# Linear attention and a sparse FFN in one kernel: some input tiles transposed through HBM instead of on TensorE, two tiles normalized on ScalarE, and finer dependences for the FFN's products

## The chip, the cores and the metric

The kernel runs on one core of a Trainium2 chip. The metric is the device time of one execution in microseconds (us). A profiled execution also gives the span from the first to the last instruction. Below, PE is TensorE, DVE is VectorE, ACT is ScalarE, POOL is GpSimd and SP is SyncE, whose queue issues nearly all DMAs.

## The reference

All is fp32. `_layernorm` has no weights.

```python
x = L0_attn_x                                       # (2, 1024, 512)
x = x + _layernorm(attn(_layernorm(x), Wq, Wk, Wv, Wo))
x = x + _layernorm(ffn(_layernorm(x), w_gate, w_up, w_down))

# attn: 16 heads of 128, 4 key/value heads; q and k rotated (RoPE), then elu(.) + 1
state = state + k_s[..., :, None] * v_s[..., None, :]      # scan over 1024 positions
z = z + k_s
out = einsum('bhe,bhed->bhd', q_s, state) / (einsum('bhe,bhe->bh', q_s, z) + EPS)
return out.reshape(...) @ Wo.T

# ffn: 512 -> 2048 -> 512
h = silu(x @ w_gate) * (x @ w_up)
h_sparse = h with the 2 largest of every 4 (by magnitude) kept, the rest zero
return h_sparse @ w_down
```

## The kernel before

**Attention.** The 1024 positions are cut into 8 chunks of 128. The two batch entries of one chunk make a "tile pair", so there are eight pairs, 0 to 7, in `xt[n]`. The heads are done in two passes of eight, so there are 16 steps `n`: pair `n % 8`, pass `n // 8`. One step of the main loop issues the Q and K/V products of step `n + 1` (`q_products`, `kv_products`), four groups of scores and outputs of step `n` (`scores`, `attend`), and the output projection of step `n - 1` (`o_products`).

**Products.** A product of 2 x 2 blocks is done with seven block products and sums of operands ahead of them (`chain`, `FACTORS`). They run in the order 1, 2, 6, 5, 7, 4, 3, in PSUM banks of three kinds: "a" (one buffer in the attention part), "b" and "e" (two each). After products 1, 6 and 7, ACT copies bank "b" out (L528), and DVE adds the copy to what stands in "a" or "e" (L539). In the trace the banks are called `ca`, `cb` and `ce`.

**x.** `step_normalize(n)` takes the layernorm of a pair on DVE (statistics L656, L661; the square root on ACT L665; L667; then the normalization L185, in place). `step_input(n, b, kind)` transposes x of one batch entry with four PE transposes (L498) into a bank. ACT copies it out (L691, L697) into the first three of the seven blocks of a tile `xf`, and DVE makes the other four (L700, L704). `xf` is stored to HBM (L707) for the second pass, which loads it again. The kernel calls `step_input(n + 2, ...)` twice in step `n`, late in the step.

**The other transposes.** From some point on q features and the attention outputs are transposed by `moved`: DVE transposes 32 x 32 blocks (L630) into a tile `blocks` of three buffers, the tile is stored to HBM (`qb`, `ob`; L636) and comes back in four loads with the blocks in their new places (`qT`, `of`; L643). The first few q tiles and the output (step 0, group 3) go over PE and bank "a" instead (`q_transposed`, copies L855; `o_transposed`, copy L1032).

**FFN.** Four blocks of 512 rows (`m`), 2048 columns in four groups (`jb`). Each `gate(m, jb)` and `up(m, jb)` is a chain whose seven products take factors of x, made by `ffn_input(m)`: the first three are views of the transposed tile (`fxr`), three are DVE sums in the tile `fxt` (L1717), one is a POOL sum in place (L1719); all four are signalled as `fxf`. `sparsify` makes the masks and the factors of h on DVE (`ht` L1507, `g` L1465), with two Abs passes on ACT (L1459) and a sum on POOL (L1510). `down(m)` is the last product (L1527).

**Who sets the order.** The kernel is written for a manual schedule: each engine executes its instructions in the order in which the program issues them. PE's order is written out in the main loop and in `ffn_order`. For all other engines a small planner (`Plan`) decides: processes yield requests such as `("dve", 0.8, rank)`, which is an engine, a planned length and a rank, or wait for a named signal, and the planner runs them by planned time. Planned lengths and signals move instructions on DVE, ACT, POOL and SP; real waits on the chip follow from the data.

Of the kernel before, what the change touches and what calls it, by code (L numbers as in the profile page):

```python
# [111 lines left out]
def kernel(  # L112
# [54 lines left out]

    fb_dram = [dram.tile([P, 4 * P], F32, name=f"fb{tt}") for tt in range(4)]
    y_dram = [dram.tile([P, B, DM], F32, name=f"y{c}") for c in range(NC)]
    x2_dram = [dram.tile([P, B, DM], F32, name=f"x2_{c}") for c in range(NC)]  # L170
# [453 lines left out]

    def moved(src, through, new, name, *names):


        yield "dve", 0.8
        t = qp.tile([P, 4, 4, 32], F32, tag="blocks", name="blocks", bufs=3)
        nc.vector.transpose(  # L630
            out=t.rearrange("p b i r -> p i b r"),
            in_=src.rearrange("p i (b d) -> p i b d", d=32),
        )
        yield 0.2
        yield "sp", 0.44
        nc.sync.dma_start(out=through, in_=t.rearrange("p b i r -> p (b i r)"))  # L636
        yield plan.transfer(256)
        for n in names:
            yield n
        for b in range(4):  # L640
            yield "sp", 0.44
            t = t if b else new()
            nc.sync.dma_start(  # L643
                out=t[b * 32 : (b + 1) * 32],
                in_=through.rearrange("(u d) (b e) -> b d u e", u=4, b=4)[b],
            )
            landing = plan.transfer(64)
        yield landing + 1.5
        plan.signal(name)
# [22 lines left out]
    def step_normalize(n, root=None, rank=1):  # L672
        yield "x", n
        scales = yield from layernorm_pair([xt[n][:, b, :] for b in range(B)], B, "a", root, rank)
        for b in range(B):
            yield "dve", 0.56, rank
            normalize(xt[n][:, b, :], xt[n][:, b, :], *scales[b])
            plan.signal(("xn", n, b))

    def step_input(n, b, kind):  # L680
# [29 lines left out]

        plan.spawn((first, second)[b]())

    def step_input_again(n):
# [79 lines left out]
    def kv_products(n):  # L793
# [18 lines left out]
        def v21(b, name):  # L812
# [9 lines left out]
            project(weights[n // NC][0], n),  # L822
            lambda i: [("xf", n), ("w", n // NC, 0, i)],
            (qp, "keep256", 2),
# [39 lines left out]
    def q_products(n):  # L864
# [20 lines left out]
        def q21(b, name):  # L885
# [6 lines left out]
            project(weights[n // NC][1], n),  # L892
            lambda i: [("xf", n), ("w", n // NC, 1, i)],
            (qp, "keep512", 2),
# [128 lines left out]

    def o_transposed(n, i):

        plan.need(("divided", n, i), *o_free(n, i))
        pt, name = transposed(o.pop((n, i)), "a", ("divided", n, i))

# [9 lines left out]
    def o_sums(n):  # L1038
# [11 lines left out]

        yield "dve", 0.8
        nc.vector.tensor_tensor(of[n, 3], of[n, 3], of[n, 0], ALU.subtract)
        plan.signal(("of", n, 3, "sum"))
        yield "dve", 0.8
        nc.vector.tensor_tensor(factor(n, 4, 1), of[n, 2], of[n, 3], ALU.subtract)
# [185 lines left out]
    def first_factors():  # L1241
# [3 lines left out]
        xnT = ffn["xnT"].rearrange("p c (w t) -> p c w t", t=32)  # L1245
        xfs[0] = ffn_factors(t, xnT, nc.vector)
        plan.signal(("fxr", 0))
        plan.signal(("fxf", 0))
# [3 lines left out]
    ORDER = (1, 2, 6, 5, 7, 4, 3)  # L1252
    wgu_loaded = set()

    def landed(length, name):
# [10 lines left out]
    def ffn_order(gate, up, down, begin, end, finish):  # L1266
# [18 lines left out]
        for k, times in ((0, 2), (1, 1), (0, 3)):  # L1285
            run(live[k], times)
        live.reverse()
        for m in range(NM):
            for jb in range(1 if m else 2, NJB):
                queue += [partial(gate, m, jb), partial(up, m, jb)]  # L1290
            if m == 1:
                live += [one() for one in queue[0:2]]
                del queue[0:2]
            weave()
            end(m)
            products = down(m)
            if m + 1 == NM:
                finish()
                run(products, 11)
                break  # L1300
            g = gate(m + 1, 0)
            if m == 0:
                run(g, 5)
            if m != 1:
# [43 lines left out]
    def gate_or_up(m, jb, which, places):  # L1348
        def multiply(b, i, start):
# [8 lines left out]
            multiply,  # L1358
            lambda i: [("fxr" if i < 3 else "fxf", m), ("gu", m, jb, which, i)],
            (pool["keeps"], "keep", 4),  # L1360
# [303 lines left out]
    def ffn_input(m):  # L1664
# [48 lines left out]
        t = pool["xs"].tile([P, 3, 2, 256], F32, tag="fxt", name="fxt")  # L1713
        v = t.rearrange("p i k (w t) -> p i k w t", t=32)
        for k, i0, i1 in ((0, b12, b11), (1, b22, v[:, 0]), (2, b21, v[:, 1])):
            yield "dve", 0.75, 0
            nc.vector.tensor_tensor(v[:, k], i0, i1, ALU.subtract)  # L1717
        yield "pool", 1.45
        nc.gpsimd.tensor_tensor(b12, b22, b12, ALU.subtract)  # L1719
        xfs[m] += [v[:, 0], v[:, 1], b12, v[:, 2]]  # L1720
        plan.signal(("fxf", m))

    E = mybir.EngineType
    with tc.manual_schedule(engines={E.PE, E.Pool, E.SP, E.DVE, E.Activation}):
# [66 lines left out]
        for n in range(STEPS):  # L1791
# [20 lines left out]
            if n + 2 < STEPS:  # L1812
                if n + 2 < NC:
                    plan.spawn(step_normalize(n + 2, ("root", n)))
                else:
                    plan.spawn(step_input_again(n + 2))
# [20 lines left out]
            else:  # L1837
# [5 lines left out]
                if n == 1:  # L1843
                    scores(1, 0)
                    q_transposed(1, 1)
                    o_transposed(0, 3)
            run(kvp, 1)
# [27 lines left out]
            else:  # L1875
# [6 lines left out]
                outputs(2)  # L1882
                if n + 2 < NC:
                    step_input(n + 2, 0, "a")
                run(opr, 2)
# [4 lines left out]
            if n > 0:  # L1890
                k_transposed(n + 1)
                run(opr, 1)
                if n + 2 < NC:
                    step_input(n + 2, 1, "a")
                outputs(3)
# [116 lines left out]
```

## Time and profile before

| | |
|---|---|
| median of 3 runs | 1292.43 us (1290.6 to 1292.5) |
| profiled execution, its own time | 1291.52 us |
| its span | 1289.8 us, mean granted PE clock 0.998 |
| busy: PE, DVE, ACT, POOL | 98%, 67%, 35%, 26% of the span |
| PE waits in all of the 1289.8 us | 23.7 us (span less busy) |
| DMA | 252.57 MB, mean 196 GB/s; 62.1% of the 16 engines' span on SP's queue |
| one step in the middle of the attention part | 42.94 us (the same score from 132.06 to 175.00 us) |

A row of a timeline reads: start us, us, engine, line, operation, output<-input, shape, count, and in brackets the idle time of the engine before it with what ended it. A line number is that of the kernel before. PE rows overlap, since matmuls are pipelined: what one costs is the distance to the next start.

### The profile page before, as it was taken

The numbers are of one execution on the slowest core, as the hardware profiler recorded it, in microseconds if no ns is written. First come the engines' busy times: TensorE is split into PE (matmuls) and PEld (weight loads), VectorE is DVE, ScalarE is ACT, GpSimd is POOL, SyncE is SP. The second block draws the span as 40 slices with busy tenths as digits, with TensorE's granted clock in tenths as the row PEclk, the third lists the DMA queues.
The fourth block names the chain that finished last, engine by engine and source line by source line (L and its number), as shares of the span: only waits on it lengthen the run. The fifth ranks groups of instructions, "written<-read, shape, count | busy, mean of one in ns | idle before, by whom it ended". The sixth has DMA issues, their size and how long they took to land. (4 is left out here: it accounts for less than half of the span.)

```text
span 1289.8 us, 17309 instructions
## 1 busy us (share of the span) xinstructions
PE 1266.1 (98%) x5868; PEld 1016.6 (79%) x5868; DVE 868.6 (67%) x1521; ACT 456.4 (35%) x905; POOL 341.1 (26%) x261
## 2 busy tenths in 40 slices
PE   7899999999999999999999999999999999999998
PEld 4567777777777777777788887888888888888886
DVE  7987876777666787678764488416981687426763
ACT  3644454444334344444443333113220333023211
POOL 4634442532232454455431101001100110110010
PEclk9999999999999999999999999999999999999999
DMA  7375678659656866676485499267547756465312
GB/s 253 116 243 197 202 232 275 208 201 313 217 191 208 295 224 229 224 235 206 156 242 166 122 261 261 92 199 217 155 124 228 237 153 199 147 184 175 114 37 95
DMA packets 280295, 252.57 MB, mean 196 GB/s; under 512 B 19216, under 2 KB 239376, under 8 KB 277520
## 3 DMA queue, kind: packets, MB, share of 16 engines
q1 hardware_dynamic: 278832, 249.51, 62.1%
q10 hardware_dynamic: 1376, 1.97, 0.4%
q8 instruction: 47, 0.77, 0.2%
q14 instruction: 40, 0.33, 0.1%
HBM read 179.83 MB, written 71.57 MB: 195 GB/s over the span
## 5 line engine op out<-in xcount | busy, mean ns | idle before, releaser
L528 ACT COPY u<-cb 128x512 f32<-128x512 f32 (+1 forms) x252 | 126.6, 503 | 477.3 <-PE cb L250 171.1
L1078 PE MATMUL cb<-wo,of 128*128 128x256 f32 x512 | 121.1, 379 | 0.0
L736 PE MATMUL cb<-wq,xf 128*128 128x512 f32 x256 | 120.4, 593 | 0.3 <-ACT u L528 0.3
L250 PE MATMUL cb<-fxnT,wgu 128*128 128x256 f32 x512 | 116.9, 379 | 2.3 <-issue 2.3
L250 PE MATMUL cb<-fxt,wgu 128*128 128x256 f32 x512 | 116.5, 379 | 0.7 <-ACT u L528 0.7
L776 POOL TENSOR_TENSOR qraw<-qraw,r 128x512 f32<-128x512 f32 x48 | 61.8, 1288 | 203.1 <-DVE qraw L767 159.8
L1078 PEld LDWEIGHTS cb<-wo,of 128*128 128x128 f32 x512 | 95.6, 190 | 23.2 <-issue 11.6
L972 ACT ACTIVATE o<-nm,den 128x128 f32<-128x128 f32 x256 | 74.0, 370 | 103.4 <-DVE state L995 82.1
L250 PEld LDWEIGHTS cb<-fxnT,wgu 128*128 128x128 f32 x512 | 97.1, 190 | 15.8 <-issue 2.7
L250 PEld LDWEIGHTS cb<-fxt,wgu 128*128 128x128 f32 x512 | 97.2, 190 | 14.3 <-ACT u L528 1.1
L1510 POOL TENSOR_TENSOR h<-h 128x512 f32<-128x512 f32 x16 | 26.1, 1632 | 287.2 <-DVE ht L1507 186.0
L449 POOL TENSOR_TENSOR wraw<-wraw 128x512 f32<-128x512 f32 x68 | 97.9, 1439 | 3.0 <-DMA of<-ob 0.4
L539 DVE TENSOR_TENSOR y<-u,ce 128x256 f32<-128x256 f32 (+1 forms) x42 | 18.9, 452 | 115.8 <-ACT u L528 57.1
L955 PE MATMUL nm<-v,am 128*128 128x129 f32 x512 | 95.4, 275 | 1.0 <-ACT o L972 1.0
L954 PE MATMUL nm<-state,qT 128*128 128x129 f32 x448 | 86.9, 276 | 0.0
L736 PEld LDWEIGHTS cb<-wq,xf 128*128 128x128 f32 x256 | 48.3, 190 | 46.6 <-issue 44.5
L955 PEld LDWEIGHTS nm<-v,am 128*128 128x128 f32 x512 | 76.4, 193 | 2.0 <-ACT o L972 1.8
L736 PEld LDWEIGHTS cb<-wkv,xf 128*128 128x128 f32 x256 | 49.5, 194 | 33.2 <-issue 27.0
L954 PEld LDWEIGHTS nm<-state,qT 128*128 128x128 f32 x448 | 72.1, 192 | 2.6
L736 PE MATMUL cb<-wkv,xf 128*128 128x256 f32 x256 | 67.2, 386 | 0.0
L910 PE MATMUL sc<-qT,kT 128*128 128x512 f32 x128 | 65.5, 594 | 0.3 <-DMA qT<-qb 0.3
L1078 PE MATMUL ce<-wo,of 128*128 128x256 f32 x256 | 60.5, 379 | 0.0
(173 smaller groups left out, 2461.4 us busy)
## 6 DMA issues: line engine op xcount, KB each, us to landing
wgu<-gs SPq DMA_DIRECT2D x64, 256.0 KB, 3.5
wgu<-us SPq DMA_DIRECT2D x64, 256.0 KB, 3.1
wd<-d_dram SPq DMA_DIRECT2D x32, 512.0 KB, 5.1
qb<-blocks SPq DMA_DIRECT2D x59, 256.0 KB, 2.3
qT<-qb SPq DMA_DIRECT2D x236, 64.0 KB, 2.2
ob<-blocks SPq DMA_DIRECT2D x58, 256.0 KB, 2.4
of<-ob SPq DMA_DIRECT2D x232, 64.0 KB, 2.2
xf<-xf SPq DMA_DIRECT2D x16, 896.0 KB, 4.8
```

Of the source, the lines that this page charges most:

```text
L250: nc.tensor.matmul(bank[:, j, :].rearrange("p (w t) -> p w t", t=32), w[:, k, j, :], xf[xi][:, k], start=(start and j == 0 and k == 0), st ...
L449: nc.gpsimd.tensor_tensor(to, i0, i1, op)
L528: nc.scalar.copy(kept[i], b)
L539: nc.vector.tensor_tensor(dst[:, rows], kept[i][:, rows], b, ALU.add)
L736: nc.tensor.matmul(bank.rearrange("p h d -> p (h d)"), xf[n][:, xi, k, :], w[wi][:, k, :], start=(start and k == 0), stop=(k == 1), skip_g ...
L776: nc.gpsimd.tensor_tensor(u, u, r, ALU.add)
L910: nc.tensor.matmul(sc.rearrange("p u h t -> p (u h t)"), kT[n][:, 2 * b + j, :], qT[n, i].rearrange("p u e -> p (u e)"), start=True, stop= ...
L954: nc.tensor.matmul(dst, q[:, u, :], state[b, j], start=True, stop=False)
L955: nc.tensor.matmul(dst, a[:, u, :], v, start=(c == 0), stop=True)
L972: nc.scalar.activation(t[:, u, :], nmv[:, u // 2, u % 2, 0:HD], AF.Copy, scale=den[:, u // 2, u % 2 : u % 2 + 1],)
L1078: nc.tensor.matmul(bank.rearrange("p h d -> p (h d)"), of[n, xi][:, k, :], weights[gp][2][wi][:, k, :], start=(start and k == 0), stop=(k ...
L1510: nc.gpsimd.tensor_tensor(b12, b22, b12, ALU.subtract)
```

## The change

1. Pairs 4 to 7: the new `step_input_moved` takes the place of `step_input`. The normalized x is transposed by DVE into two unused blocks of the `xf` tile, stored to HBM (`xb`), loaded back over x itself, copied into `xf` by ACT and summed by DVE. It starts right after the normalization, and the normalization of these pairs does not wait for the signal "root" (given in the middle of the step's products) any more. With `blocks` given, `moved` allocates no buffer.
2. Pairs 2 and 3: the normalization runs on ACT, as `x * rs + shift`, with `shift = -mean * rs` from DVE.
3. The output of step 0, group 3, is transposed into bank "e" instead of "a". The first two `of` sums get rank 0.
4. The first products of K/V and Q wait, in the planner, for `xf0` (the copies) alone, the others for `xf` (all).
5. FFN: each product waits, in the planner, for its own sum (`fxs`), and the first gate product of block 1 is put among the last up products of block 0.

```diff
+    xb_dram = [[dram.tile([P, 4 * P], F32, name=f"xb{k}{b}") for b in range(B)] for k in range(2)]
...
-    def moved(src, through, new, name, *names):
+    def moved(src, through, new, name, *names, blocks=None):
         yield "dve", 0.8
-        t = qp.tile([P, 4, 4, 32], F32, tag="blocks", name="blocks", bufs=3)
+        t = blocks or qp.tile([P, 4, 4, 32], F32, tag="blocks", name="blocks", bufs=3)
...
     def step_normalize(n, root=None, rank=1):
         scales = yield from layernorm_pair([xt[n][:, b, :] for b in range(B)], B, "a", root, rank)
+        if n in (2, 3):
+            shift = small.tile([P, B], F32, tag="shift", name="shift")
+            for b in range(B):
+                mean, rs = scales[b]
+                yield "dve", 0.12, rank
+                nc.vector.scalar_tensor_tensor(
+                    shift[:, b : b + 1], mean, -1.0, rs, ALU.mult, ALU.mult
+                )
         for b in range(B):
-            yield "dve", 0.56, rank
-            normalize(xt[n][:, b, :], xt[n][:, b, :], *scales[b])
+            x_ = xt[n][:, b, :]
+            if n in (2, 3):
+                yield "act", 0.65, rank
+                nc.scalar.activation(
+                    x_, x_, AF.Identity, bias=shift[:, b : b + 1], scale=scales[b][1]
+                )
+            else:
+                yield "dve", 0.56, rank
+                normalize(x_, x_, *scales[b])
             plan.signal(("xn", n, b))
...
+    def step_input_moved(n):
+        t = ln.tile([P, 7, 2, P], F32, tag="xf", name="xf")
+        xf[n] = t
+        both = all_of(2, ("xf0", n))
+        def tile_in(b):
+            yield "xn", n, b
+            x_ = xt[n][:, b, :]
+            to = x_.rearrange("p (u i r) -> p u (i r)", u=4, r=32)
+            yield from moved(
+                x_.rearrange("p (c d) -> p c d", c=NIC), xb_dram[n % 2][b], lambda: to,
+                ("xm", n, b),
+                blocks=t[:, 3 + 2 * b : 5 + 2 * b].rearrange("p q k (i r) -> p (q k) i r", r=32),
+            )
+            yield 5.0
+            v = x_.rearrange("p (u i r) -> p i u r", u=4, r=32)
+            if b == 0:
+                yield "act", 0.65
+                nc.scalar.copy(t[:, 0:2].rearrange("p q k (u r) -> p (q k) u r", r=32), v)
+            else:
+                yield "act", 0.4
+                nc.scalar.copy(t[:, 2].rearrange("p k (u r) -> p k u r", r=32), v[:, 2:4])
+            both()
+            if b == 1:
+                yield "xf0", n
...
+        for b in range(B):
+            plan.spawn(tile_in(b))
...
-            lambda i: [("xf", n), ("w", n // NC, 0, i)],
+            lambda i: [("xf0" if i < 3 and n < NC else "xf", n), ("w", n // NC, 0, i)],
...
-        yield "dve", 0.8
+        yield "dve", 0.8, 0
         nc.vector.tensor_tensor(of[n, 3], of[n, 3], of[n, 0], ALU.subtract)
...
+    FX = {
+        i: partial(lambda k, m: ("fxs", m, k) if k < 3 else (("fxr", "fxf")[k - 3], m), k)
+        for i, k in {1: 3, 2: 3, 3: 3, 4: 2, 5: 0, 6: 1, 7: 4}.items()
+    }
...
+        def one_of_gate():
+            nonlocal g
+            g = gate(1, 0)
+            yield
+            yield next(g)
...
+            if m == 0:
+                queue.append(one_of_gate)
             weave()
...
-            lambda i: [("fxr" if i < 3 else "fxf", m), ("gu", m, jb, which, i)],
+            lambda i: [FX[i](m), ("gu", m, jb, which, i)],
...
-                    plan.spawn(step_normalize(n + 2, ("root", n)))
+                    plan.spawn(step_normalize(n + 2, None if n > 1 else ("root", n)))
+                    if n > 1:
+                        step_input_moved(n + 2)
...
-                    o_transposed(0, 3)
+                    o_transposed(0, 3, "e")
...
-                if n + 2 < NC:
-                    step_input(n + 2, 0, "a")
+                if n == 1:
+                    step_input(3, 0, "a")
```

PE's order is the same but for three things: the x transposes of pairs 4 to 7 are gone, the o group is in `ce`, and the one gate product of FFN block 1 stands earlier. On the other engines many instructions change places.

More of the change, by code (lines that the diff above doesn't have):

```diff
@@ L711, in step_input @@
         plan.spawn((first, second)[b]())
+    def step_input_moved(n):
[7 more added lines that the diff above has]
+            yield from moved(
+                x_.rearrange("p (c d) -> p c d", c=NIC),
+                xb_dram[n % 2][b],
+                lambda: to,
+                ("xm", n, b),
+                blocks=t[:, 3 + 2 * b : 5 + 2 * b].rearrange(
+                    "p q k (i r) -> p (q k) i r", r=32
+                ),
+            )
[10 more added lines that the diff above has]
+                yield "xf0", n
+                yield "dve", 0.45
+                nc.vector.tensor_tensor(
+                    t[:, 3].rearrange("p k (u r) -> p k u r", r=32),
+                    v[:, 0:2],
+                    t[:, 0].rearrange("p k (u r) -> p k u r", r=32),
+                    ALU.subtract,
+                )
+                for to_, i0, i1 in ((4, 2, 3), (5, 4, 0), (6, 1, 4)):
+                    yield "dve", 0.45
+                    nc.vector.tensor_tensor(t[:, to_], t[:, i0], t[:, i1], ALU.subtract)
+                plan.signal(("xf", n))
+                yield "sp", 0.44, 2
+                nc.sync.dma_start(out=xf_dram[n], in_=t)
+                plan.transfer(896)
+                plan.signal(("xf stored", n))
+        for b in range(B):
+            plan.spawn(tile_in(b))
     def step_input_again(n):
@@ L892, in q_products @@
             project(weights[n // NC][1], n),
-            lambda i: [("xf", n), ("w", n // NC, 1, i)],
+            lambda i: [("xf0" if i < 3 and n < NC else "xf", n), ("w", n // NC, 1, i)],
             (qp, "keep512", 2),
@@ L1022, in o_free, with o_transposed @@
         return names + ([("of", k, 6)] if i == 2 and k >= 0 else [])
-    def o_transposed(n, i):
+    def o_transposed(n, i, kind="a"):
         plan.need(("divided", n, i), *o_free(n, i))
-        pt, name = transposed(o.pop((n, i)), "a", ("divided", n, i))
+        pt, name = transposed(o.pop((n, i)), kind, ("divided", n, i))
         def copy():
@@ L1049, in t3 @@
             plan.signal(("of", n, 5))
-        yield "dve", 0.8
+        yield "dve", 0.8, 0
         nc.vector.tensor_tensor(of[n, 3], of[n, 3], of[n, 0], ALU.subtract)
         plan.signal(("of", n, 3, "sum"))
-        yield "dve", 0.8
+        yield "dve", 0.8, 0
         nc.vector.tensor_tensor(factor(n, 4, 1), of[n, 2], of[n, 3], ALU.subtract)
@@ L1246, in first_factors @@
         xfs[0] = ffn_factors(t, xnT, nc.vector)
+        for k in range(3):
+            plan.signal(("fxs", 0, k))
         plan.signal(("fxr", 0))
@@ L1287, in ffn_order @@
         live.reverse()
+        g = None
+        def one_of_gate():
[3 more added lines that the diff above has]
+            yield next(g)
         for m in range(NM):
@@ L1300, in ffn_order @@
                 break
-            g = gate(m + 1, 0)
             if m == 0:
-                run(g, 5)
+                run(g, 4)
+            else:
+                g = gate(m + 1, 0)
             if m != 1:
@@ L1714, in ffn_input @@
         v = t.rearrange("p i k (w t) -> p i k w t", t=32)
+        xfs[m] += [v[:, 0], v[:, 1], b12, v[:, 2]]
         for k, i0, i1 in ((0, b12, b11), (1, b22, v[:, 0]), (2, b21, v[:, 1])):
@@ L1717, in ffn_input @@
             nc.vector.tensor_tensor(v[:, k], i0, i1, ALU.subtract)
+            plan.signal(("fxs", m, k))
         yield "pool", 1.45
         nc.gpsimd.tensor_tensor(b12, b22, b12, ALU.subtract)
-        xfs[m] += [v[:, 0], v[:, 1], b12, v[:, 2]]
         plan.signal(("fxf", m))
@@ L1892 @@
                 run(opr, 1)
-                if n + 2 < NC:
-                    step_input(n + 2, 1, "a")
+                if n == 1:
+                    step_input(3, 1, "a")
                 outputs(3)
```

## The prediction

> **What bounds the kernel now.** I read the page first: busy time by engine, and the span in 40 slices.
>
> ```profile
> PE 1266.1 (98%) x5868; PEld 1016.6 (79%) x5868; DVE 868.6 (67%) x1521; ACT 456.4 (35%) x905; POOL 341.1 (26%) x261
> ```
>
> TensorE (PE) is busy 98% of 1289.8 us, so the time falls only if PE has less to do or waits less. The page's chain that ended last covers only the tail after 1285 us. So I next asked who PE waits for (total us, times, longest):
>
> ```profile
> PE ca L498 <- DVE x L185: 7.5, 1, 7.5
> PE cb L250 <- issue: 2.3, 1, 2.3
> PE ca L736 <- ACT of L1032: 2.0, 1, 2.0
> PE ca L498 <- DVE qraw L784: 1.5, 1, 1.5
> PE ca L498 <- ACT qT L855: 1.4, 2, 0.8
> PE nm L955 <- ACT o L972: 1.0, 1, 1.0
> PE cb L250 <- ACT u L528: 0.7, 1, 0.7
> ```
>
> The 7.5 us is the start, which nothing here touches. Every other wait of weight lies before 80 us or near 800 us. From 80 to 660 us PE never waits. Third, the timeline of PE around the 2.0 us wait, and the windows there (length, then busy us of PE, PEld, DVE, ACT, POOL, granted clock, DMA share, GB/s):
>
> ```profile
> 71.66 0.66 PE L498 MATMUL ca<-ident,qraw 128*128 128x128 f32 x4
> 72.99 0.66 PE L498 MATMUL ca<-ident,o 128*128 128x128 f32 x4 [0.68 <-ACT qT L855]
> 75.60 2.08 PE L736 MATMUL ca<-wkv,xf 128*128 128x256 f32 x4 [1.95 <-ACT of L1032]
> 77.47 0.64 PE L954 MATMUL nm<-state,qT 128*128 128x129 f32 x2
> ```
> ```profile
> 75.60:77.47 1.87, 1.87 (x5) 1.51 (x5) 0.65 (x2) 1.84 (x3) 1.70 (x2) 0.50 0.22 84
> 77.47:79.00 1.53, 1.53 (x11) 1.53 (x10) 1.29 (x3) 0.22 (x1) 0.00 (x0) 0.65 0.48 138
> ```
>
> Three users queue for the only buffer of bank "ca"; each waits for ACT to copy the one before out. After the second gap the clock is at half. Fourth, a normal step:
>
> ```profile
> 186.48 1.02 PE L910 MATMUL sc<-qT,kT 128*128 128x512 f32 x2
> 187.34 0.60 PE L498 MATMUL ca<-ident,x 128*128 128x128 f32 x4
> 187.78 1.89 PE L1078 MATMUL cb<-wo,of 128*128 128x256 f32 x8
> ```
>
> One x transposition costs PE 187.78 - 187.34 = 0.44 us on the path (starts, not the overlapping durations). Last, the wait near 804 us, called "issue": PE first, then ACT.
>
> ```profile
> 802.30 1.89 PE L250 MATMUL ce<-fxt,wgu 128*128 128x256 f32 x8
> 806.48 1.97 PE L250 MATMUL cb<-fxnT,wgu 128*128 128x256 f32 x8 [2.30 <-issue]
> ```
> ```profile
> 803.91 2.00 ACT L1459 ACTIVATE s<-h 128x1024 f32<-128x1024 f32 x2 [4.28 <-DVE h L1455]
> 805.82 0.57 ACT L528 COPY u<-cb 128x512 f32<-128x512 f32 x1
> ```
>
> PE starts 0.09 us after the copy of `cb` ends (806.39). That copy, due at about 802.3, stood behind two Abs activations that waited for DVE.
>
> **Part 1: x of pairs 4 to 7 through HBM.** It removes 8 groups of 4 PE transposes: 8 x 0.44 = 3.5 us of path. PE has no wait in 80-660 us, so all of it counts if nothing new is late. It adds 8 DVE stream transposes (8 x 0.70 = 5.6 us, rows of L630), 8 stores (2.3 us to landing, as `qb`) and 32 loads (2.2 us, as `qT`): 40 issues of about 0.44 us, 4.4 us of SP per step of 42.9 us. ACT's copies and DVE's sums stay; their source is SBUF. On DVE's new order the normalization and both transposes (1.0 + 1.4 us) fall, in the first of these steps, between 158 and 161 us, where DVE idles 3.82 us for PE; in the next, 1.4 us falls in a hole of 1.52 us. On SP the eight loads fall after `qb`, `ob` at 173.2 us; SP then has nothing until 180.2 us, and the eight take 3.5 us. They are moved ahead of that step's `qT` loads, whose users are 7 us or more away (landed by 158.5, used at 166.1). The chain of one x: scale ready 158.2, transposed 160.8, stored by 164.3, loaded by 179.3, copied by ACT near 187, summed by 194. The first products want the copies at 157.2 + 42.9 = 200.1 us, the sums at 204. It hides with 13 and 10 us to spare; uncovered, each us costs four. Bounds: 2.0 (DVE windows near 220 and 260 us are 92-94% busy) to 3.9; I take 3.5, the row itself. One rule speaks against this part: the Trainium skill, "VectorE: DVE Perf Modes", section "Rules for kernel authors", would leave a 128x128 transposition on TensorE if PSUM will do. By it this part brings nothing, and the sum would end 3.5 us higher. I go by the row: 0.44 us each on a saturated PE.
>
> **Part 2: pairs 2 and 3 normalized on ScalarE, o through bank "e", early order.** DVE loses 3.06 us (46.31, two L185 beside a busy POOL) and 1.00 us (82.45), and gains four [128,1] operations of about 0.15 us. ACT gains 4 x 0.63 us (row of L779). Followed by hand on the new orders: at 47.4 us ACT does 1.3 us of x, so the `qT` copy that ended at 51.18 us ends near 52.5; PE wants it for the score at 51.51: a new wait of 1.1 us, with the next K and Q products queued behind. It replaces rather than adds: the 0.76 us for a later `qT` copy (57.17) goes, and since DVE's masks and divisors come earlier, `nm` at 62.96 starts near 62.3. Then `ca`: the o group goes to `ce`, whose two buffers were freed at 68.9 and 63.7 us, so the K/V product waits only for the `qT` copy, done at about 72.7 (ACT still has `r` and `u` before it). It starts at 72.8 instead of 75.60: 2.8 us. The idle gap shrinks to about 0.9 us, and gaps of 1.48 us (44.07) and 1.00 us (62.96) left the clock at 1.00. So the half clock goes: this product took 1.87 us from start to start against 0.86 for the same at 80.86, the next three `nm` starts 0.43, 0.43, 0.33 against 0.22: 1.0 + 0.5 = 1.5 us. Together 4.3 us. Next late would be the mask for `nm`, by my count at 72.9, with PE there at 73.7. Bounds: 1.5 (the copy is held up by 1.3 us, one L776 on POOL, and the clock still falls) to 5.1 (no gap at all). By the Trainium skill, "TensorE: Matmul & The Clock Gate", Part 1, the clock falls only after an idle window of about 3.4 us; by that the 1.5 us would not be there to win, and the sum would be 7.8. The trace shows 0.50 after gaps of 0.68 and 1.95 us, so I count it.
>
> **Part 3: FFN products wait for their own sums.** Only one PE group moves: the first gate product of block 1 goes ahead of the up product that waited 0.73 us at 793.56, and covers that. ACT's order now puts the `cb` copy ahead of the two Abs, so the 2.30 us goes. What is late next: DVE's order now has two `ht` sums (2.4 us beside POOL, as at 762.59) ahead of the `fxt` sums; the second `fxt` sum ends near 801.2 instead of 799.8, while PE comes at 799.6: a new wait of 1.7 us. 0.73 + 2.30 - 1.7 = 1.3; with the 0.2 us of slow first matmuls after the two gaps, 1.5. Bounds: 0 (both `ht` and the first `fxt` slowed by POOL) to 3.0. The other order changes (sums of `of` with a higher rank, copies in the last attention steps) move work by under 2 us where PE comes 4 us or more later: nothing.
>
> **Sum.** 3.5 + 4.3 + 1.5 = 9.3 us against the profiled execution's own 1291.52 (1289.8 and 1.7 around it): 1282.2. The median of the runs, 1292.43, lies 0.9 above that execution; I add half: 1282.7. About 0.2%, 2.6 us, is what can be told from no change.
>
> **Rivals.**
> A. *DVE turns the 3.5 us into waits.* For it: slices of 18.7 busy us in 20. Against: the slices between have 10.6 to 13. It leaves 5.8 us: 1286.2.
> B. *The early gain is lost:* a mask or `kf` is late instead of the bank. For it: DVE is 88-95% busy up to 80 us, and my hand count has 0.8 us of slack there. It leaves 5.0 us: 1287.0.
> C. *Slower:* SP issues in order; a store that waits for DVE holds the eight x loads and everything behind. One group of `of` loads took 4.94 us at 164.72 so. It decides once the x chain slips by more than 13 us: four steps then lose the excess each. At 16.5 us that is 4 x 3.5 - 9.3 = +4.7: 1296.7. Against: the loads have 7 us of empty queue after them.
> D. *Part 3 does nothing that PE feels,* since data dependences order it on the chip anyway: 1284.2, inside the range.
>
> **Numbers.** Forecast 0.68 with D inside it, A 0.09, B 0.12, C 0.07, the rest (about no change) 0.04. All low bounds give 2.0 + 1.5 + 0 = 3.5, so 1288.0; all high ones 3.9 + 5.1 + 3.0 = 12, so 1279.5. That takes in A and B and leaves out C and the rest. Faster by over 0.2%: 0.68 + 0.09 + 0.12 = 0.89; the same 0.04; slower 0.07.
>
> **What would show it.** Right: in PE's waits the rows `ACT of L1032` and "issue" are gone, a wait of about 1 us for `qT` stands near 51.5 us, the clock is 1.00 from 60 to 80 us, steps 2 to 5 take 42.0 us instead of 42.9, and one wait under 2 us remains at the start of FFN block 1. Wrong: any PE wait between 80 and 300 us on `xf`, on `am` or on `qT` loads, or a clock row of 0.5 near 75 us.

## The result, and the profile after

The changed kernel takes 1295.22 us (median of 9 runs, 1294.25 to 1298.2), the kernel before 1291.18 us beside it (9 runs). The ratio is 1.0031, 95% interval 1.0022 to 1.0041: 4.0 us slower, where 9.7 us less was forecast. The profiled execution took 1295.22 us, its span is 1293.4 us. Lines of the changed kernel are 2 higher than before up to some L650 (L498 is now L500) and 67 higher in the attention part (L910 is now L977, L1078 is L1145).

PE's waits in the changed kernel, in the same columns as in the prediction:

```profile
PE sc L977 <- DMA qT<-qb: 4.0, 1, 4.0
PE cb L1145 <- ACT u L530: 2.4, 2, 1.6
PE ce L1145 <- DVE y L541: 2.0, 2, 1.4
...
PE cb L252 <- issue: 1.0, 1, 1.0
...
PE sc L977 <- ACT qT L922: 0.9, 1, 0.9
```

The rows `ACT of L1032` (2.0 us) and "issue" with 2.3 us are gone, as forecast. The first three rows are new. Their waits lie between 181 and 258 us, where PE never waited before. These are PE's rows at the place of the old 1.95 us wait, and at the longest new one:

```profile
73.72 1.13 PE L803 MATMUL ca<-wkv,xf 128*128 128x256 f32 x4 [0.58 <-ACT qT L922]
...
257.78 1.33 PE L977 MATMUL sc<-qT,kT 128*128 128x512 f32 x2 [3.98 <-DMA qT<-qb]
```

The windows of the kernel before, then of the changed kernel (length, then busy us of PE, PEld, DVE, ACT, POOL, granted clock, DMA share, GB/s):

```profile
60.00:80.00 20.00, 16.36 (x69) 10.38 (x68) 17.59 (x31) 12.09 (x26) 9.84 (x9) 0.91 0.78 244
160.00:180.00 20.00, 20.00 (x84) 12.95 (x83) 12.86 (x27) 9.95 (x21) 5.90 (x5) 1.00 0.81 271
180.00:200.00 20.00, 20.00 (x113) 17.14 (x112) 18.80 (x35) 8.78 (x21) 11.79 (x9) 1.00 0.67 215
```
```profile
60.00:80.00 20.00, 18.34 (x81) 11.48 (x80) 18.65 (x38) 12.36 (x31) 10.26 (x9) 1.00 0.83 260
160.00:180.00 20.00, 20.00 (x92) 14.34 (x91) 8.34 (x19) 7.47 (x17) 4.92 (x4) 1.00 0.94 290
180.00:200.00 20.00, 16.10 (x87) 12.87 (x86) 19.20 (x33) 6.89 (x17) 13.69 (x10) 1.00 0.60 186
240.00:260.00 20.00, 15.43 (x61) 10.33 (x60) 14.77 (x32) 7.89 (x17) 5.01 (x4) 0.96 0.84 291
```

The row of 60 to 80 us is the gain: clock 1.00 instead of 0.91, and PE 2 us busier. The others are the loss. DVE is 42% busy in 160 to 180 us and 96% in the next 20; the kernel before has 64% and 94% there, and PE does not stand. So the high share alone is not what PE waits for: DVE does less early, and its work comes late. The DMA share in 160 to 180 us is 0.94, where the kernel before has 0.81.

The account, from the starts of the same score in both traces. At the score near 80 us the changed kernel is 3.3 us ahead (76.70 against 80.00). The four steps in which x is moved take 42.06, 47.04, 50.51 and 42.06 us (128.82, 170.88, 217.92, 268.43, 310.49 us); the same steps took 42.94, 42.94, 43.15 and 42.94. At the last score it is 5.9 us behind (685.85 against 679.92), at the end of the span 3.6. So it won 3.3 us early, 3.5 us of transposes and 2.3 us after the last score, and lost 5.9 + 3.3 + 3.5 = 12.7 us. Of these, 9.7 us are waits and 1.8 us the slow clock behind the 3.98 us gap (10.65 us to the next score, 8.89 before). I have not assigned the last 1.2 us.

**The chain behind the waits of 181 to 198 us.** First DVE in the changed kernel:

```profile
179.27 0.69 DVE L1119 TENSOR_TENSOR of<-of 128x512 f32<-128x512 f32 x1 [7.58 <-DMA of<-ob]
...
180.61 0.68 DVE L989 TENSOR_TENSOR am<-sc,causal 128x512 f32<-128x512 f32 x1
```

DVE stands 7.58 us for a load of `of`. Everything behind that sum on DVE stands too: the mask `am` that PE wants at 180.7 us, then the sums that free PSUM. Next SP, which issued the load:

```profile
161.28 4.54 SPq L645 DMA_DIRECT2D of<-ob  x4
165.92 0.41 SPq L638 DMA_DIRECT2D ob<-blocks  x1
166.43 3.59 SPq L645 DMA_DIRECT2D qT<-qb  x4
170.06 0.43 SPq L427 DMA_DIRECT2D wraw<-in_w_gate_dram  x1
170.59 1.86 SPq L638 DMA_DIRECT2D xb<-xf  x2
...
173.03 2.04 SPq L645 DMA_DIRECT2D of<-ob  x4
```

And the same part of SP's queue in the kernel before:

```profile
160.50 0.34 SPq L636 DMA_DIRECT2D ob<-blocks  x1
...
164.72 4.94 SPq L643 DMA_DIRECT2D of<-ob  x4
171.76 0.40 SPq L425 DMA_DIRECT2D wraw<-in_w_gate_dram  x1
```

Two things changed. The `ob` store, though its transpose ended on DVE at 156.30 us, stands behind another group of `of` loads. And its own loads are now behind a 1024 KB load of weights and both x stores, so they leave at 173.03 us instead of 164.72, though the changed kernel is 4.1 us ahead at the score of this step (170.88 against 175.00); before, they were ahead of the weights. Once issued, they take about as long to land as before (median 5.0 us, before 5.4): they are late because they leave late.

**The chain behind the wait at 257.78 us** is another one. SP in the changed kernel:

```profile
245.36 0.43 SPq L453 DMA_DIRECT2D us<-wraw  x1
249.94 0.38 SPq L427 DMA_DIRECT2D wraw<-in_w_up_dram  x1
250.43 0.45 SPq L638 DMA_DIRECT2D qb<-blocks  x1
250.97 2.43 SPq L645 DMA_DIRECT2D qT<-qb  x4
```

SP stood 4.1 us until the store of `us` had read its tile, before it could load that tile again. The transposed q features behind it were ready at 245.7 us. In the kernel before, the last `qT` loads went out at 241.16 us, ahead of the store of `us` at 243.81.

### The profile page after: what moved, and what is told of

The parts are those of the page before. It is cut to its first block, busy times and chain, and to the rows that moved or that the text cites. A ratio compares the mean times of both kernels' runs of the same rounds, so it can differ in the third digit from the quotient of the medians.

```text
span 1293.4 us, 17294 instructions
## 1 busy us (share of the span) xinstructions
PE 1263.2 (98%) x5836; PEld 1012.6 (78%) x5836; DVE 865.6 (67%) x1529; ACT 457.1 (35%) x909; POOL 337.3 (26%) x261
## 5 line engine op out<-in xcount | busy, mean ns | idle before, releaser
L1145 PE MATMUL cb<-wo,of 128*128 128x256 f32 x512 | 121.2, 379 | 2.4 <-ACT u L530 2.4
L1145 PEld LDWEIGHTS cb<-wo,of 128*128 128x128 f32 x512 | 95.9, 190 | 27.7 <-issue 12.2
L977 PE MATMUL sc<-qT,kT 128*128 128x512 f32 x128 | 66.0, 597 | 4.9 <-DMA qT<-qb 4.0
L1145 PE MATMUL ce<-wo,of 128*128 128x256 f32 x256 | 60.7, 380 | 2.0 <-DVE y L541 2.0
```

The lines of the kernel that those rows point to most:

```text
L977: nc.tensor.matmul(sc.rearrange("p u h t -> p (u h t)"), kT[n][:, 2 * b + j, :], qT[n, i].rearrange("p u e -> p (u e)"), start=True, stop= ...
L1145: nc.tensor.matmul(bank.rearrange("p h d -> p (h d)"), of[n, xi][:, k, :], weights[gp][2][wi][:, k, :], start=(start and k == 0), stop=(k ...
```

## The experiments

Each kernel was timed against the kernel before on the same chip, so ratios are compared; 0.0010 is 1.3 us. "Waits" are PE's in 100 to 300 us of the profile, "of" is DVE's longest standing there for the `of` loads. They come from one execution each: that of p1_only (1297.67 us, median 1301.59) and that of g2_late_wraw (1294.35, median 1297.40) are the fastest of theirs, that of e2_no_rank (1299.94, median 1296.76) is the slowest.

| run | ratio (95%) | us against before | waits, us | of, us |
|---|---|---|---|---|
| changed kernel | 1.0031 (1.0022-1.0041) | +4.0 | 9.7 | 7.6 |
| e1_no_x | 0.9970 (0.9958-0.9982) | -3.9 | 0.0 | 2.7 |
| e2_no_rank | 1.0038 (1.0026-1.0050) | +4.9 | 6.9 | 5.9 |
| e3_no_x_no_rank | 0.9972 (0.9961-0.9984) | -3.6 | 0.5 | 2.5 |
| p1_only | 1.0074 (1.0058-1.0089) | +9.6 | 4.4 | 6.4 |
| p2_only | 0.9987 (0.9977-0.9997) | -1.7 | 1.0 | 3.0 |
| p3_only | 0.9972 (0.9961-0.9984) | -3.6 | 0.0 | 2.4 |
| f2_dma_alone | 1.0001 (0.9992-1.0011) | +0.1 | 1.8 | 3.3 |
| f3_dve_alone | 0.9966 (0.9954-0.9978) | -4.4 | 1.7 | 3.9 |
| f4_quarter | 1.0008 (0.9995-1.0022) | +1.0 | 8.0 | 6.1 |
| f5_root | 1.0035 (1.0022-1.0048) | +4.5 | 10.9 | 4.4 |
| g1_act_queue | 1.0097 (1.0084-1.0110) | +12.5 | 13.4 | 11.8 |
| g2_late_wraw | 1.0038 (1.0023-1.0054) | +4.9 | 1.1 | 4.9 |
| g3_pairs_4_7 | 1.0011 (0.9999-1.0022) | +1.4 | 6.2 | 8.2 |
| g4_pair_7 | 0.9960 (0.9946-0.9974) | -5.2 | 0.3 | 3.3 |
| h2_phantom | 0.9985 (0.9974-0.9995) | -1.9 | 3.7 | 4.1 |
| h4_same_order | 1.0015 (1.0002-1.0028) | +1.9 | 5.1 | 5.9 |
| h5_same_order_early | 1.0018 (1.0009-1.0027) | +2.3 | 5.7 | 5.6 |
| h6_same_order_quarter | 0.9996 (0.9986-1.0007) | -0.5 | 3.6 | 5.5 |

PE waits 3.6 us or more when DVE stands over 5 us for `of`, and at most 1.8 below 4; f5_root, g2_late_wraw and h2_phantom lose in other ways (below). Some also wait behind this stretch: e2_no_rank, p1_only and g2_late_wraw have one wait of 3.7 to 4.1 us each for `y` between 327 and 335 us.

### Which part of the change

**e1_no_x**: the changed kernel with x back on PE.

```diff
-                    plan.spawn(step_normalize(n + 2, None if n > 1 else ("root", n)))
-                    if n > 1:
-                        step_input_moved(n + 2)
+                    plan.spawn(step_normalize(n + 2, ("root", n)))
...
-                if n == 1:
-                    step_input(3, 0, "a")
+                if n + 2 < NC:
+                    step_input(n + 2, 0, "a")
```

> The changed kernel with x of pairs 4 to 7 transposed on PE again; all else as changed. After the change the trace has 12.7 us of new waits and slow clock between 165 and 290 us, against 3.5 us of PE transposes that are gone; up to 80 us it has gained 3.3 us, and after 680 us 2.3 us. Theory 1 (the x transfers hold SP's in-order queue, the loads of `of` come late, DVE stands for them at its `of` sums): all new waits go, 1291.2 - 3.3 - 2.3 = 1285.6 us, and DVE's wait for `of` falls from 18.6 us in 80 to 300 us to about 3. Theory 2 (DVE has too much to do beside POOL in 180 to 240 us): the same 1285.6, since the eight DVE transposes go too. Theory 3 (the higher rank of the `of` sums alone makes DVE stand in the wrong place): the waits stay, 1295 to 1298 us.

0.9970, and no PE wait between 100 and 300 us. All of the loss comes with part 1: it costs 1.0031 - 0.9970, 7.9 us, where the prediction had it bring 3.5. Theory 3 is out. The other parts bring 3.9 us, not 5.6. DVE's wait for `of` in 100 to 300 us falls from 18.6 to 6.8 us, not to 3. Theories 1 and 2 are not told apart by this run.

**e2_no_rank**: the changed kernel with the old rank of the sums.

```diff
-        yield "dve", 0.8, 0
+        yield "dve", 0.8
         nc.vector.tensor_tensor(of[n, 3], of[n, 3], of[n, 0], ALU.subtract)
```

> The changed kernel with the two `of` sums at their old rank; x still goes through HBM. Theory 1: the loads of `of` are as late as before this edit, but fewer masks and sums stand behind them on DVE; a part of the 12.7 us stays, 1287 to 1293 us. Theory 2: DVE has the same work, 1295 us. Theory 3: all waits go and the 3.5 us of PE transposes stay won, 1295.2 - 12.7 = 1282.5 us.

1.0038: no gain. DVE still stands for `of` (5.9 us at most, 17.4 in all, against 18.6). PE's wait for `qT` falls from 4.0 to 1.0 us, but waits of 1.9 us for `kf` and of 4.1 us for `y` at 334.30 us are new. What stands first behind the sum matters little.

**e3_no_x_no_rank**: both undone, by the two diffs above.

> Both undone: x of pairs 4 to 7 on PE, the `of` sums at their old rank; left are pairs 2 and 3 normalized on ScalarE, the o group in bank e, and the FFN edits. All three theories: 1291.2 - 3.3 - 2.3 = 1285.6 us, with no PE wait between 80 and 660 us. If the rank also matters without the x transfers, this differs from the kernel that has only x undone by more than 1 us.

0.9972, the same as e1_no_x: the rank does nothing without the transfers.

**p1_only**: the kernel before with x through HBM and `xf0` alone.

```diff
+                    plan.spawn(step_normalize(n + 2, None if n > 1 else ("root", n)))
+                    if n > 1:
+                        step_input_moved(n + 2)
```

> The kernel before with x of pairs 4 to 7 through HBM and the early `xf0` signal, and nothing else of the change. Theory 1: PE saves 3.5 us, the loads of `of` come late, part of the 12.7 us of waits appears: 1291 to 1297 us. Theory 2: the whole 12.7 us appears, 1291.2 - 3.5 + 12.7 = 1300 us. Theory 3: no new wait without the new rank, 1291.2 - 3.5 = 1287.7 us.

1.0074, 9.6 us slower, without any other part. In the terms of the text (1291.2 x 1.0074 = 1300.8) that is theory 2's number and over theory 1's range; theory 2 falls with f3_dve_alone below, so part of this loss I had not foreseen. Its trace has 4.4 us of waits in 100 to 300 us and a further 3.7 us for `y` near 333 us.

**p2_only** (pairs 2 and 3 on ScalarE, bank "e", `xf0`) and **p3_only** (the FFN's edits), each on the kernel before.

```diff
+        if n in (2, 3):
+            shift = small.tile([P, B], F32, tag="shift", name="shift")
...
-                    o_transposed(0, 3)
+                    o_transposed(0, 3, "e")
...
-            lambda i: [("xf", n), ("w", n // NC, 0, i)],
+            lambda i: [("xf0" if i < 3 and n < NC else "xf", n), ("w", n // NC, 0, i)],
```

> The kernel before with part 2 alone: pairs 2 and 3 normalized on ScalarE, the o group in bank e, the early signal `xf0`. By the prediction's step 4.3 us less; by the trace of the changed kernel, which has gained 3.3 us at the score near 80 us, 3.3 less: a ratio of 0.9974. If that gain is lost again later, 1.000.

```diff
-            lambda i: [("fxr" if i < 3 else "fxf", m), ("gu", m, jb, which, i)],
+            lambda i: [FX[i](m), ("gu", m, jb, which, i)],
...
+            if m == 0:
+                queue.append(one_of_gate)
             weave()
```

> The kernel before with part 3 alone: FFN products wait, in the planner, for their own sums, and one gate product moves. By the prediction's step 1.5 us less, by the trace of the changed kernel 2.0 to 2.3 less: a ratio of 0.9982 to 0.9988. If data dependences order it on the chip anyway, 1.000.

p2_only is at 0.9987, 1.7 us won (0.4 to 3.0). Between the first score (41.01 us) and the one at 78.84 us it wins the expected 3.2 us; but it reaches the first score 2.0 us later than the kernel before (38.98), and a new wait of 1.00 us for `kT` at 150.54 us takes the rest: at 153.05 us it is level with the kernel before (152.91). For the first loss its PE and DVE rows show why:

```profile
27.17 0.63 PE L500 MATMUL ca<-ident,x 128*128 128x128 f32 x4 [2.14 <-issue]
```
```profile
25.77 1.75 DVE L187 TENSOR_SCALAR x<-x,mv,rs 128x512 f32<-128x512 f32 x2
```

The normalization of pair 1 began at 23.11 us in the kernel before. Now the sum and the rotation of k and a sum of `wq` weights stand ahead of it on DVE, and PE, due with x's transposes, waits. The wait varies: 0.89 us in the changed kernel's profile, 0.67 to 2.60 in those of the other kernels with part 2.

p3_only is at 0.9972, 3.6 us won (2.1 to 5.0), nearly all that e1_no_x wins with all parts but part 1. Its trace shows 2.3 us of it between the last score and the end; the two waits of 0.73 and 2.30 us became one of 1.01.

### What of x's way costs

**f2_dma_alone** and **f3_dve_alone**: x on PE, and beside it only the transfers, or only the DVE transposes, into parts of `xf` that are overwritten later.

```diff
+            yield "sp", 0.44
+            nc.sync.dma_start(out=xb_dram[n % 2][b], in_=xt[n][:, b, :])
+            yield plan.transfer(256)
+            for k in range(4):
+                yield "sp", 0.44
+                nc.sync.dma_start(out=to[k * 32 : (k + 1) * 32], in_=...)
```

> x of pairs 4 to 7 is transposed on PE as in the kernel with only x undone (1287.6 us), but x is also stored to `xb` and loaded from it, with as many DMAs and bytes as in the change, into parts of `xf` that are overwritten later; DVE does not transpose x. It prices the transfers without DVE's work. Theory 1 (transfers in SP's in-order queue make the loads of `of` late): most of the cost of 7.6 + 3.5 = 11.1 us comes back, 1295 to 1299 us, with DVE waits for `of` of over 10 us in 140 to 300 us. Theory 2 (DVE has too much to do): 1287.6 us.

```diff
+            yield "dve", 0.8
+            to = t[:, 3 + 2 * b : 5 + 2 * b].rearrange("p q k (i r) -> p (q k) i r", r=32)
+            nc.vector.transpose(out=to.rearrange("p b i r -> p i b r"), in_=...)
```

> x of pairs 4 to 7 on PE, but DVE also does the two block transposes of x per step, early, as in the change, into parts of `xf` that are overwritten later; no transfer of x. Theory 1: the eight transposes of 0.7 us fall in holes, 1287 to 1289 us. Theory 2: 1295 to 1299 us.

DVE's transposes alone cost nothing (0.9966 beside 0.9970): theory 2 is out as the whole cause. The transfers alone cost 4.0 us (1.0001), under half of the 11.1 expected, and DVE stands 3.3 us for `of` at most.

**f4_quarter**: a quarter of the bytes in the same DMAs and the same order.

```diff
+        rows = slice(0, 32 if blocks is not None else P)
-        nc.sync.dma_start(out=through, in_=t.rearrange("p b i r -> p (b i r)"))
+        nc.sync.dma_start(out=through[rows], in_=t.rearrange("p b i r -> p (b i r)")[rows])
...
+            us = slice(0, 1 if blocks is not None else 4)
-                out=t[b * 32 : (b + 1) * 32],
+                out=t[b * 32 : (b + 1) * 32, us],
```

> The changed kernel, with the same DMAs of x in the same order, but each moves a quarter of the rows (x is then only partly transposed). It tells SP's order from the load on the DMA engines. If the places in SP's queue make the `of` loads late: as the changed kernel, 1294 to 1296 us. If the bytes on the DMA engines do: the waits shrink by about three quarters of what x costs, 1285 to 1288 us. Theory 2: 1295 us.

1.0008: 3.0 us come back, under half of what the bytes theory asks. The wait for `qT` near 256 us is still there, with 4.22 us, and DVE still stands 6.1 us.

**f5_root**: x normalized late, so that its stores go behind the `of` loads.

```diff
-                    plan.spawn(step_normalize(n + 2, None if n > 1 else ("root", n)))
+                    plan.spawn(step_normalize(n + 2, ("root", n)))
```

> The changed kernel, with the normalization of pairs 4 to 7 waiting for the signal root again, so that on SP the stores of x stand behind the loads of `of` that DVE needs first, and the loads of x behind the next `qT` loads. The same DVE work and the same bytes. Theory 1: the waits for `of` go, 1291.2 - 3.3 - 2.3 - 3.5 = 1282 to 1286 us if x still comes in time. Theory 2: 1295 us.

1.0035: a miss for theory 1 as I had put it. DVE's standing falls to 4.4 us, but now PE waits 7.17 us for `qT` at 215.48 us: DVE had transposed it by 199.5 us, but its store left at 204.61 us, behind eight `of` loads that took SP 7.07 us, and its loads began at 209.83 us.

**g1_act_queue**: x's DMAs from ScalarE's queue.

```diff
-        yield "sp", 0.44
-        nc.sync.dma_start(out=through, in_=t.rearrange("p b i r -> p (b i r)"))
+        queue, of_ = (nc.sync, ("sp", 0.44)) if blocks is None else (nc.scalar, ("act", 0.1))
+        yield of_
+        queue.dma_start(out=through, in_=t.rearrange("p b i r -> p (b i r)"))
...
-            yield "sp", 0.44
+            yield of_
...
-            nc.sync.dma_start(
+            queue.dma_start(
```

> The changed kernel with the stores and loads of x issued from ScalarE's queue instead of SyncE's; planned 1 and 2 us later, so that ScalarE should rarely stand for them. Same bytes, same DVE work. Theory 1a (x holds SP's in-order queue): the waits of the changed kernel go and the saved transposes show, 1282 to 1286 us. Theory 1b (the bytes crowd the DMA engines, which carry 94% in 160 to 180 us): little changes, 1292 to 1296 us. If ScalarE itself stands at the new DMAs, PE waits for `u` or `qT` copies and it is over 1296 us.

1.0097, by far the slowest, and over the ranges of theories 1a and 1b. ScalarE stands little for the new DMAs: its waits name `x<-xb` with 1.7 us in the whole run. SP's do (165 to 190 us; total us, times, longest):

```profile
SPq L646 <- DMA x<-xb: 11.4, 3, 5.7
```

L646 issues the loads of `moved`, which on SP are `qT` and `of`; neither reads x. In the trace every DMA signals one of eight semaphores, 100 to 107, shared by both queues, and no DMA is issued before the one that last used its semaphore has landed: in all 20 profiles at most eight DMAs are under way at a time. The `of` load issued at 184.84 us uses semaphore 100; so did x's load of 180.04 us, which landed at 184.83. So SP still stands for x, now for x's landings. DVE stands 11.8 us for these `of` loads, and PE then waits 8.67 us.

The run says little about the bytes. The `ob` store at 167.84 us took 9.0 us to land, but 2 MB of other transfers were issued in the 1.9 us before it; in the kernel before, with no x on the way, the `ob` store at 173.22 us, behind a 1024 KB load of weights, took 7.5. The Trainium skill, "DMA: Bandwidth & Descriptors", section "Issuing engines are not separate DMA queues", says that DMAs of any issuing engine run on the same 16 DMA engines and interleave; this run agrees: in 165 to 185 us SP's queue takes 64.5% of the 16 engines' time and ScalarE's 13.1%.

### The links of the chain

**g2_late_wraw**: prepared weights loaded 6 us later in the plan.

```diff
             if n + 1 < len(units):
+                if n > 0:
+                    yield 6.0
                 loaded = yield from load_unit(n + 1)
```

> The changed kernel with one more planned delay: each prepared block of weights after the second is loaded 6 us later. In the changed kernel SP stood 4.1 us at the load of w_up near 246 us until the store of `us` had read its tile, with the store of `qb` behind it whose loads PE waited 4.0 us for at 257.78 us. If that standing is the link, the 4.0 us and the 1.8 us of slow clock after it go: 1289 to 1291 us. If the q features were late by DVE's backlog alone, 1294 to 1296 us.

The 4.0 us wait near 257 us is gone, as the link asks, and so are most of the waits of 181 to 243 us (1.1 us are left in 100 to 300 us), since the delay moves other DMAs too. But the time is 1.0038: the new order has other waits, 3.89 us for `y` at 328 us and 1.4 us for `qT` at 667 us.

**g3_pairs_4_7** and **g4_pair_7**: x through HBM for two pairs, or one (`(7,)` in place of `(4, 7)`).

```diff
-                    if n > 1:
+                    if n + 2 in (4, 7):
                         step_input_moved(n + 2)
...
-                if n == 1:
-                    step_input(3, 0, "a")
+                if n + 2 < NC and n + 2 not in (4, 7):
+                    step_input(n + 2, 0, "a")
```

> The changed kernel with x through HBM for pairs 4 and 7 alone (transfers near 126 to 138 us and 257 to 269 us); pairs 5 and 6 on PE. In the changed kernel the waits came after the transfers of pairs 5 and 6 (171 to 181 us and 215 to 223 us). If those two alone cost: 1287.6 (only x undone) less 4 x 0.44 = 1285.8 us. If each pair costs alike: 1287.6 + 7.6 / 2 = 1291.4 us.

> x through HBM for pair 7 alone, pairs 4 to 6 on PE. If the last pair costs nothing, 1287.6 - 2 x 0.44 = 1286.7 us; if each pair costs alike, 1287.6 + 7.6 / 4 = 1289.5 us.

Pair 7 alone costs nothing: 0.9960, beside 0.9970 for no pair. I had thought from the place of the waits that pair 4 is free too; it is not: with it the ratio is 1.0011. Its profile has DVE standing 8.2 us for `of` and one PE wait of 5.09 us at 182.91 us, though no x moves between 140 and 250 us there.

### Order or work

g3_pairs_4_7 points at the planner: x's work in the plan gives other instructions new places. These runs separate that. "x free" would be e1_no_x less 3.5 us: 0.9943. It is no run but a sum; g4_pair_7 fits it (0.9960 measured, 0.9963 for e1_no_x less 2 x 0.44 us).

**h2_phantom**: the changed kernel's order, x's transposes and transfers planned but left out (the diff shows the store; the transpose and the loads are the same).

```diff
-        nc.sync.dma_start(out=through, in_=t.rearrange("p b i r -> p (b i r)"))
+        if blocks is None:
+            nc.sync.dma_start(out=through, in_=t.rearrange("p b i r -> p (b i r)"))
```

> The changed kernel's order of all instructions, but the DVE transposes, stores and loads of x of pairs 4 to 7 are left out (these pairs go on untransposed); the planner still counts them. Copies and sums of x stay. Theory P (the planner's new order of the other instructions makes the `of` loads late): as the changed kernel, 1293 to 1297 us. Theory W (the work of x itself, its issues and bytes): the saved transposes show and no wait is left, 1291.2 - 3.3 - 2.3 - 3.5 = 1282 to 1285 us.

0.9985, between both theories: 5.4 us over "x free". Its only PE wait in 100 to 300 us, and what SP did before it:

```profile
250.92 1.10 PE L980 MATMUL sc<-qT,kT 128*128 128x512 f32 x2 [3.73 <-DMA qT<-qb]
```
```profile
238.74 0.43 SPq L453 DMA_DIRECT2D us<-wraw  x1
243.14 0.38 SPq L427 DMA_DIRECT2D wraw<-in_w_up_dram  x1
243.63 0.45 SPq L640 DMA_DIRECT2D qb<-blocks  x1
```

This is the wait at 257.78 us of the changed kernel, with SP standing in the same place, and no x moves at all. The order alone makes it; with the slow clock behind it (0.73 in the next 3 us) it is most of that difference. The waits of 181 to 243 us are gone here, and DVE stands at most 4.1 us.

**h4_same_order** and **h5_same_order_early**: all instructions as in e1_no_x, x's work put in at no planned length, with its stores behind or ahead of the last `of` loads.

```diff
+        seen = 1.0 if blocks is None else 0.0
-        yield "dve", 0.8
+        yield "dve", 0.8 * seen
...
-        pt, name = transposed(xt[n][:, b, :]..., kind, ("xn", n, b))
+            plan.pe(0.45, lambda: None, *before, ("xn", n, b))
```

> All instructions in the order of the kernel with only x undone (1287.6 us); PE's x transposes are left out, and x's DVE transposes, stores and loads are put in at no planned length, the stores behind the loads of `of` that DVE needs first. Full work of x, right result. Theory P: 1287.6 - 3.5 = 1283 to 1285 us. Theory W: the transfers still crowd SP and the DMA engines, 1291 to 1296 us.

The second run differs from the first in this alone:

```diff
-                    plan.spawn(step_normalize(n + 2, ("root", n)))
+                    plan.spawn(step_normalize(n + 2, None if n > 1 else ("root", n)))
```

> As the run before, but with x normalized early as in the change, which puts x's stores ahead of the last `of` loads of each step on SP. Theory P: 1283 to 1287 us. Theory W: 1292 to 1296 us. If only the place ahead of `of` costs, the run before is at 1284 and this one over 1288 us.

1.0015 and 1.0018, theory W's numbers: 9.3 and 9.7 us over "x free". The wait for `qT` is gone, the waits behind late `of` loads are there:

```profile
DVE of L1102 <- DMA of<-ob: 13.2, 4, 5.9
```

This is h4_same_order's row of DVE's waits in 100 to 300 us (total us, times, longest); e1_no_x has 6.8 us there, the changed kernel 18.6. Whether x's stores go ahead of the `of` loads or behind makes no difference.

**h6_same_order_quarter**: as h4_same_order, a quarter of the bytes, by the diff of f4_quarter.

> The kernel with the old order and x's work put in at no planned length, each DMA of x moving a quarter of its rows (x only partly transposed). With all bytes it was at 1.0015 of the kernel before; with x's work free it would be at 0.9943 (0.9970 less 3.5 us). If the bytes on the DMA engines cost: 0.994 to 0.997, 1286 to 1289 us. If the places in SP's queue cost: 1.000 to 1.002, 1293 to 1295 us.

0.9996, 2.5 us less than with all bytes; the two intervals overlap a little, but f4_quarter shows the same (3.0 us). Three quarters of the bytes carry about a quarter of the cost; the rest stays with the issues and their chains. Which of these, and by how much, is not settled. One candidate is the eight semaphores of g1_act_queue: in 100 to 300 us SP's stores and loads of `moved` stand 8.7 us in the changed kernel for DMAs that they do not need (`xf`, `y`, weights and others), and 3.5 us in h2_phantom, which has the same order without x. No run changes their number. Nor is it settled why the transfers cost 4.0 us beside PE's transposes (f2_dma_alone) and 9.3 with DVE's in their place (h4_same_order).

**Taken together.** Against "x free", the order alone costs 5.4 us, the work in the old order 9.3, both 11.4. They do not add up; I take it that a wait that one makes is often there for the other. The fastest versions leave x on PE, for all pairs or for all but the last: e1_no_x and g4_pair_7 beat both kernels, and are not told apart.

## Why the prediction was wrong, by its own steps

**Part 1 failed: -3.5 us forecast, +7.9 measured.** The arithmetic of x itself held: PE lost its eight groups, steps without new waits took 42.06 us (42.0 forecast), and no PE wait for `xf` shows in any profile. The step that failed is the one from "It hides with 13 and 10 us to spare" to 3.5 us: x did hide, but what x and its place in the plan make late was put at nothing, and cost 11.4 us against "x free". I followed x's chain and asked whether x would be late. I did not ask what x makes late. Two of the prediction's own signs of being wrong came: PE waits of 0.6 us on `am` and of 4.0 us on `qT` loads. Three sentences were at fault:

- "SP then has nothing until 180.2 us". It was idle because its next load waited 6.5 us for the store of `qb` to land, not because there was room. The DMA share in 160 to 180 us was 0.81, and x took it to 0.94.
- "whose users are 7 us or more away". It weighs the `qT` loads behind x's loads, and not the `of` loads behind x's stores. The user of those is a sum on DVE with all of DVE's work behind it.
- "The other order changes ... nothing". The order alone costs 5.4 us, most of it the wait of 3.73 us in h2_phantom (3.98 in the changed kernel) and its slow clock. I looked at moves by their length on the engine, and on SP one place can mean standing 4.1 us for a tile to come free.

Rival A named where the waits would show, at DVE, but put it down to DVE's load; the eight transposes alone cost nothing. Rival C named SP's order and the sign. It gave the wrong condition: it decided when x slips by 13 us, and x never slipped. Its row was misread, too: no store waited for DVE ahead of the `of` loads that took 4.94 us (the `ob` store had left at 160.50 us, and SP's waits in 150 to 182 us name DVE with 0.5 us at most). That its price, 4 x 3.5 = 14 us, was near the 12.7 that were lost, and its 1296.7 us near the result, is luck. The rule that spoke against this part gave the better advice, though not for DVE's time: the loss comes with the way through HBM.

**Part 2: right mechanism, half the size in the end.** The wait for the bank went, the `qT` copy became late by 0.88 us at 52.70 us (1.1 at 51.5 forecast), and the product started at 73.72 us at clock 1.00 (72.8 forecast). Near 80 us 3.3 of the 4.3 us had come. But the term has no line for the wait at 27 us, nor for the 1.00 us at 150.54 us; measured alone, it leaves 1.7 us (0.4 to 3.0). I followed the new orders by hand from 44 us on, and the signal `xf0` had moved DVE's work before that.

**Part 3: right, undersized.** One wait of 1.01 us is left, 1.7 forecast, so the trace gives 2.0 to 2.3 us where 1.5 stood; alone it measured 3.6 (2.1 to 5.0). Rival D is out.

**The clock.** I went by the row, 0.50 behind gaps of 0.68 and 1.95 us, against the rule. With the gap at 0.58 us the clock stayed at 1.00 in 60 to 80 us, as forecast. But the gap does not fix it: p1_only has the same gap of 1.95 us, at 76.52 us, and its clock stayed at 1.00. So part of the 1.5 us counted for the clock is chance. The other gaps are below.

## What to carry to other kernels

Moving work from a full engine to an idle one is priced by what the new work delays, not by whether it comes in time itself: list for every in-order queue it joins (SP, the DMA engines, DVE) what stands behind it, and follow the chain that already ends last there. Count the DMAs as well as the bytes: with a quarter of the bytes, about three quarters of the cost stayed. An issue queue that is idle in the trace may be waiting, and is then no free room. Where a planner sets the order, measure the order and the work apart: leave the work out at the same order, and put it in at the old order.

## What the runs showed of the hardware

The clock by the length of PE's gap, in 20 profiles, the start and the end aside (granted clock in the 3 us that follow): gaps of 1.20 to 1.80 us left it at 1.00 every time. Of gaps from 1.85 to 3.67 us some left it at 1.00 (1.95, 2.23, 2.30, 3.67 us) and some did not (1.85: 0.67, 1.95: 0.51, 2.10: 0.57, 2.14: 0.64, 2.23: 0.64, 2.60: 0.52, 3.19: 0.53); 1.95 and 2.23 us did both. Gaps of 3.73 to 8.67 us always lowered it to 0.50 to 0.73. Each slow stretch is at 0.50 throughout and lasts 3.41 us (75.14 to 78.55 us in the kernel before), 6.83 or 10.24, once, twice or three times as long. The Trainium skill, "TensorE: Matmul & The Clock Gate", Part 1, has a free-running window of about 3.4 us after which an idle PE is slowed. The length of the stretches agrees, and a window at a chance position would fit the mixed range, but these runs show falls after gaps well below its length.

At most eight DMAs were under way at a time in each of the 20 profiles, over both queues, and a DMA stood until the one that last used its semaphore had landed. A second issuing queue did not free SP of x: SP stood 11.4 us for x's loads in 165 to 190 us of g1_act_queue.

A store of 256 KB took 2.5 us to land, and 7.5 us behind a 1024 KB load of weights, in one trace (`ob`, 160.50 and 173.22 us of the kernel before). A DMA's time from a row of one trace holds only for the queue and the traffic of that place.
